# Layer-norm statistics of a gated cross-attention block: totals over partitions on TensorE, or on VectorE after copies by ScalarE

## The chip, the cores and the metric

The kernel runs on one core of a Trainium2 chip. A core has five engines that run side by side, each through its own instructions in order: TensorE for matrix products (PE in the profile; its weight loads are shown apart as PEld), VectorE (DVE), ScalarE (ACT), GpSimd (POOL) and SyncE (SP), which issues most DMAs. They wait for one another through semaphores. Working data lie in SBUF, products land in PSUM (eight banks); both have 128 partitions.

The metric is device time in microseconds (us): the median of three runs, and beside it one profiled execution from which all durations come.

## What is computed

`x` is 4 x 2048 tokens of 512 features, the context 4 x 77 rows of 384. Without the drawing of inputs and the splitting into 16 heads of 64 the reference is:

```python
def _layernorm(x, axis=-1, eps=1e-05):
    m = jnp.mean(x, axis=axis, keepdims=True)
    v = jnp.var(x, axis=axis, keepdims=True)
    return (x - m) / jnp.sqrt(v + eps)

# attention: softmax((x Wq)(ctx Wk)^T / 8) (ctx Wv) Wo + bo, softmax over the 77 context rows
x = x + jnp.tanh(g_xattn[0]) * _L0_xattn_ref(_layernorm(x, axis=-1), ctx_768, Wq, Wk, Wv, Wo, bo)
# FFN: one of eight matrices, picked by argmax(log_softmax(logits) + gumbel(u)): x W[idx] + b[idx]
x = x + jnp.tanh(g_ffn[0]) * _L0_ffn_ref(_layernorm(x, axis=-1), W, b, logits, u)
```

So every token is normalised twice: before the attention (here "x statistics") and before the FFN ("y statistics", of the attention's result).

## The kernel before, in words

**Weights are folded.** Wq and the keys are multiplied ahead into `m`, one matrix per batch row from the 512 features to 16 heads x 80 padded context rows; Wv and Wo into `vo`. Wq and W are centred, so the mean of a token need not be subtracted from it, and 1/std is applied after the product. What the norm has to deliver is therefore 1/std of each token: `rs`, and for the softmax `up` and `down`, 1/std times plus and minus 1/8.

**Groups.** The 8192 tokens go in 16 groups of 512. In the loop `for i in range(1, NGRP)` (from L802), step i computes the scores of group i, the attention of group j = i - 1 and the FFN of j, whose last product and row work fall into the next step, where that group is called f. Each of these is a Strassen-like product of seven block products instead of eight: class `Seven` (L458). `product(s)` puts block product s on PE, and `post(s)` moves a finished sum from PSUM. By `ORDER` (L460), products 0, 2, 4 and 6 add up in bank r = 0, products 1 and 5 in r = 1, product 3 in r = 2. Posts 0, 1, 2 and 6 are copies by ACT (`keep`, L485 or L489), posts 3, 4 and 5 additions by DVE into the copies in `snap` (L504). Since product 4 adds onto what is in bank 0, it can start only when post 2 has copied that bank; product 2 likewise waits for post 0, product 5 for post 1. The last group's attention and FFN use the order `BY_TOKENS`, where product 3 adds onto the bank that post 1 copies and product 4 onto that of post 2.

**Order.** The schedule is written by hand: each engine runs its instructions in the order in which the program lists them, so an instruction that waits holds all behind it on its engine.

**Layout and statistics.** A row tile holds 512 tokens: partition 32a + c holds feature piece a (128 of the 512 features) of tokens c, c + 32, and so on, 16 tokens along the free axis. `bn_stats` on DVE (L375) gives for each partition and token two triples (count, mean, 64 times the variance) of the even and the odd elements. Each token's eight means and eight variances thus lie on four partitions, 32 apart, and must be combined over them. The class `Norms` (L361) does it in four steps:

- `mean`: DVE adds the two means (L379), and PE multiplies with `jm` (L384), a constant of 0.125 wherever the partitions agree modulo 32. Each partition then has the token's mean, in the PSUM bank `stat`.
- `spread` and `var`: DVE subtracts it from the piece means, squares, adds the variances (L399 to L403) and adds pairs (L379); PE multiplies with `jm` again (L384).
- `rstd`: DVE adds eps (L412), POOL raises to the power -0.5 (L415 for x, L422 for y) and makes `down` and `up` (L418, L419).

`apart` separates DVE's additions from the product (`flush`), so that PE need not wait. There are 19 such objects: groups 0 and 1 before the loop (x only, n = 16 columns), groups 2 to 15 in the loop (y of group f and x of group i together, n = 32), and three at the end (the y of group 14, n = 16, and the two halves of group 15, `n1` and `n0`, n = 8).

**Where they stand.** For groups 0 and 1 the steps are in the loop over `s1` of group 0 (L710 to L733), which also centres and scales the FFN weights (`centre_wf`, `scale_wf`: L655 to L663). In the loop, `mean` comes after the seventh product of `s0` (L844) and the other steps at s = 1 to 3 of the scores `s1` and `s2` (L848). At the end they are in the last attention (L970 to L982, and L998 to L1000) and in the last FFN (L1026 to L1045). There the FFN rows are scaled by `rs` (L1018 on ACT, L1063 on DVE) and added to `y` (L1022, DVE), and the result is stored by halves.

Of the kernel before, what the change touches and what calls it, by code (L numbers as in the profile page):

```python
# [8 lines left out]
F32 = mybir.dt.float32  # L9
U32 = mybir.dt.uint32  # L10
AF = mybir.ActivationFunctionType
ALU = mybir.AluOpType
AX = mybir.AxisListType
# [6 lines left out]
def flamingo_block_kernel(  # L20
# [79 lines left out]
    tq = cp.tile([P, 4, NDC // 2, T2], F32, tag="tq")  # L100
    bo_c = cp.tile([P, NDC], F32, tag="bo_c")
    bf_r = cp.tile([P, P], F32, tag="bf_r")
    jm = cp.tile([P, NA, 32], F32, tag="jm")
    ones = cp.tile([P, P], F32, tag="ones")
    neghalf = cp.tile([P, NG], F32, tag="neghalf")
    snap = cp.tile([P, NCC * ID], F32, tag="snap")
# [79 lines left out]

    nc.gpsimd.memset(neghalf, -0.5)
    nc.gpsimd.memset(ones, 1.0 / D)
    nc.gpsimd.memset(jm, 0.0)
    for a in range(NA):  # L190

        for a2 in range(NA):
            nc.gpsimd.affine_select(
                out=jm[:, a, :], in_=jm[:, a, :], compare_op=ALU.not_equal, fill=0.125,
                base=-32 * a2, pattern=[[-1, 32]], channel_multiplier=1)

    def by_chunk(t):

# [162 lines left out]
    class Norms:  # L361


        apart, waiting = False, None

        def __init__(self, i, n=None):
            self.y = 2 <= i
            self.x = i < NGRP
# [5 lines left out]
            for g in range(g0, g0 + n):  # L374
                nc.vector.bn_stats(self.s6[:, at + g, :], t[:, g, :])  # L375

        def total(self, pairs, half):
            t = small.tile([P, self.n], F32, tag=f"tot{half}", name="tot")
            nc.vector.tensor_reduce(t, pairs, AX.X, ALU.add)  # L379
            self.waiting = half, t  # L380

        def flush(self):
            half, t = self.waiting
            nc.tensor.matmul(self.ps[:, half], jm.rearrange("p a c -> p (a c)"), t, start=True, stop=True)  # L384

        def mean(self):
            n = self.n
            self.ps = stat[:, : 2 * n].rearrange("p (h n) -> p h n", h=2)
            self.mm = self.s6.rearrange("p g (h s) -> p g h s", h=2)
            self.total(self.mm[:, :, :, 1], 0)  # L390
            if not self.apart:
                self.flush()

        def spread(self):
            n = self.n
            sq = stat[:, ds(4 * NG, 2 * n)].rearrange("p (n h) -> p n h", h=2)
            dv = small.tile([P, n, 2], F32, tag="dv", name="dv")
            for t in (dv, sq):
                nc.vector.tensor_tensor(t, self.mm[:, :, :, 1],  # L399
                                        self.ps[:, 0].unsqueeze(2).to_broadcast([P, n, 2]), ALU.subtract)  # L400
            nc.vector.tensor_tensor(sq, sq, dv, ALU.mult)
            self.q = small.tile([P, n, 2], F32, tag="q", name="q")
            nc.vector.scalar_tensor_tensor(self.q, self.mm[:, :, :, 2], 1.0 / 64, sq, ALU.mult, ALU.add)  # L403

        def var(self):
            self.total(self.q, 1)
            if not self.apart:
                self.flush()

        def rstd(self):  # L410
            self.rs = small.tile([P, self.n], F32, tag="rs", name="rs")
            nc.vector.tensor_scalar(self.rs, self.ps[:, 1], EPS, None, ALU.add)  # L412
            if self.x:
                r = self.rs[:, ds(self.x0, NG)]
                nc.gpsimd.tensor_tensor(r, r, neghalf, ALU.pow)  # L415
                self.up = small.tile([P, NG], F32, tag="up", name="up")
                self.down = small.tile([P, NG], F32, tag="down", name="down")
                nc.gpsimd.tensor_scalar(self.down, r, -SCALE, None, ALU.mult)  # L418
                nc.gpsimd.tensor_scalar(self.up, r, SCALE, None, ALU.mult)  # L419
            if self.y:  # L420
                r = self.rs[:, : min(self.n, NG)]
                nc.gpsimd.tensor_tensor(r, r, neghalf[:, : min(self.n, NG)], ALU.pow)  # L422

    def to_columns(dst, src, q):
        nc.vector.transpose(dst[:, q, :].rearrange("p (g c) -> p g c", c=32), src[:, :, ts(q, 32)])  # L425
# [112 lines left out]
    nmx = {}  # L538

    def head_max(i, h):  # L540
        mx = stat[:, ds((8 + h) * NG, NG)]
        nc.vector.tensor_reduce(mx, head(i, h), AX.X, ALU.max)  # L542
        nmx[h] = small.tile([P, NG], F32, tag=f"nmx{h}", name="nmx")
        nc.vector.tensor_tensor(nmx[h], mx, norms[i].down, ALU.mult)  # L544
# [127 lines left out]
        ff.post(6)  # L672

    def norm_step(n, s):
        if s < 4:
            (n.mean, n.spread, n.var, n.rstd)[s]()

    def early_step(n, s):

        if s == 0:  # L680
            n.apart = True
            n.mean()
        elif s == 1:
            n.flush()
            n.spread()
            n.var()
        elif s == 2:
            n.flush()
            n.rstd()


    n = norms[0]
# [17 lines left out]
    for s in range(7):  # L710
        s1.product(s)
        if s == 0:
            s1.post(0)
            s0.product(6)
            s0.post(6)
            early_step(n, 0)
            for k in range(2):
                s_rows(0, KH + k, s0.chunk(1, k))
            sum_wf(wfr)
        elif s < 3:  # L720
            early_step(n, s)
            n1.stats(xg[1], 0, 8 * (s - 1), 8)
        elif s < 6:
            early_step(n1, s - 3)
        if 0 < s:
            s1.post(s)
        if s == 4:
            centre_wf(wfr)
        if s == 5:
            scale_wf(wfr)  # L730
            for k in range(2):
                s_rows(0, 2 + k, s1.chunk(0, k))
# [69 lines left out]
    for i in range(1, NGRP):  # L802
# [4 lines left out]
        if 1 < i:  # L807

            s0 = scores0(i)
            for s in range(6):  # L810
                s0.product(s)
                if s == 0:
                    s0.post(0)
                    if 0 <= f:
                        end_of_ff(f)
                    p_columns(j, 6, 8)
                    xc[i].sum("T4")
                if s == 1:
                    p_columns(j, 8, 10)
                    if 0 <= f:  # L820
                        f_rows(f, ff, 1)
                if s == 2:
                    pT[j].sum("T1")
                    pT[j].sum("T3")
                if 0 < s:
                    s0.post(s)
                if 0 <= f and s in (2, 3):
                    n.stats(ys[f], 0, 8 * (s - 2), 8)
                if s == 3 and 0 <= f:
                    add_bias(f, nc.gpsimd)  # L830
            for k in range(2):
                s_rows(i, k, s0.chunk(0, k))

# [2 lines left out]
            for s in range(7):  # L836
                s1.product(s)
                s2.product(s)
                if s == 0:
                    s1.post(0)  # L840
                    s2.post(0)
                    s0.product(6)
                    s0.post(6)
                    n.mean()  # L844
                    for k in range(2):
                        s_rows(i, KH + k, s0.chunk(1, k))
                elif s < 4:
                    norm_step(n, s)  # L848
                if swap_vo and 3 <= s:
                    weight_sum(vo, s - 3, nc.vector if s < 5 else None)  # L850
                if 5 <= s and 0 <= f:
# [108 lines left out]
    for s in range(7):  # L960
# [7 lines left out]
            pT[j].sum("T3")  # L968
            n.stats(ys[f], 0, 0, NG)
        if s == 1:  # L970
            n.apart = True
            n.mean()
            add_bias(f, nc.vector)
        if s == 2:
            n.flush()
            n.spread()
            n.var()
            pT[j].sum("T4")
        if s == 3:
            n.flush()  # L980
            n.rstd()
            f_scale(f, n.rs, 0, 8)  # L982
        if s == 4:
            residual(j, at, "12")
# [9 lines left out]
        if s == 6:  # L994
            yc[j].sum("T3")
            residual(j, at, "11")
            y_rows(j, 2, 1)
            n1.stats(ys[j], -8, 8, 8)  # L998
            n1.apart = n0.apart = True
            n1.mean()  # L1000
            y_rows(j, 0, 0)
            residual_last(j, at)
    yc[j].sum("T1")
# [13 lines left out]
        for g in range(NG // 2):  # L1017
            nc.scalar.activation(d[:, g, :], d[:, g, :], AF.Copy, scale=rs[:, g : g + 1])  # L1018

    def added(h, v):  # L1020
        y = by_feature(ys[j], h, v)
        nc.vector.tensor_tensor(y, y, by_feature(ts_[j], h, v), ALU.add)  # L1022

    for s in range(6):
        ff.product(s)
        if s == 0:  # L1026
            n1.flush()
            n1.spread()
            n1.var()
            y_rows(j, 2, 0)  # L1030
            n0.stats(ys[j], 0, 0, 8)
        if s == 1:
            n1.flush()
            n1.rstd()
            yc[j].sum("T4")
            n0.mean()
            half_bias(1, nc.vector)
        if s == 2:
            n0.flush()
            half_bias(0, nc.gpsimd)  # L1040
            n0.spread()
            n0.var()
        if s == 3:
            n0.flush()
            n0.rstd()  # L1045
        ff.post(s)
        if s == 3:
            f_rows(j, ff, 0, 1)
            scaled(0, 1, n1.rs)
        if s == 4:  # L1050
            f_rows(j, ff, 1, 1)
            added(0, 1)
            scaled(1, 1, n1.rs)
        if s == 5:
            f_rows(j, ff, 0, 0)
            scaled(0, 0, n0.rs)
            added(1, 1)
            store(j, 8, 8, (nc.sync, nc.sync, nc.sync, nc.scalar))
    ff.product(6)
    for k in range(2):  # L1060
        to_rows(ts_[j], ff.ps[0][:, k, :], 2 + k, 0)
    d = by_feature(ts_[j], 1, 0)
    nc.vector.tensor_tensor(d, d, n0.rs.unsqueeze(2).to_broadcast(list(d.shape)), ALU.mult)  # L1063
    added(0, 0)
    added(1, 0)
    store(j, 0, 8, (nc.sync, nc.scalar))


# [39 lines left out]
```

## Time and profile before

| | |
|---|---|
| Three runs | 1263.02, 1263.13, 1263.99 us; median 1263.13 |
| The profiled execution | 1261.51 us; span from first to last instruction 1259.6 us; granted TensorE clock 0.998 |
| Statistics products on PE (L384) | 38 products, 76 records, 0.256 us median each |
| Powers on POOL | L415: 16 of 128x16, median 2.91 us, longest 4.09; L422: 15 of 128x16, 2.93; 2 of 128x8, 2.71 and 1.65 |
| Small operations of `spread` (128x64) on DVE | L399 0.20 and 0.23, L401 0.23, L403 0.24, L379 0.22 us |
| A small copy on ACT (L310, 128x80) | 0.23 us long, the next copy starts after 0.12 |
| DVE's addition of 128x512 (L1022), POOL's (L576) | 0.69 us, 1.27 us |
| One group of the loop, from product to same product | 72.97 us |

The page divides the span into 40 slices of 31.5 us and gives each engine's busy share in tenths; "PEclk" is the clock granted to TensorE, 9 meaning full speed. The chain of work that ended last is followed back from the last instruction, at each step to what released it. A row of a timeline gives start, duration, engine, line, operation, what is written and read, the shapes, how many like instructions are merged, and in brackets how long the engine was idle before and what ended that.

### The profile page before, as it was taken

Reading aid. Unit: us, or ns where it says so; the run is one execution under the profiler, and the core shown is the slowest. Engines: PE = TensorE matmul, PEld = TensorE weight load, DVE = VectorE, ACT = ScalarE, POOL = GpSimd, SP = SyncE. Lnnn points to the kernel's source line nnn. Section 1 sums busy time; section 2 is a strip of 40 time slices with the busy share of each in tenths; the row PEclk is TensorE's granted clock in tenths of the full one; section 3 lists DMA queues with packets and bytes.
Section 4 is the critical chain, followed back from the end, with each engine's and each line's share of the span. In section 5 each row is a group of like instructions: output and inputs, shape, how many; then the busy total and the mean of one; then the engine's idle time right before and its main releaser. Section 6 shows DMA issues by size and latency. Waiting matters only on the chain.

```text
span 1259.6 us, 16932 instructions
## 1 busy us (share of the span) xinstructions
PE 1246.9 (99%) x5780; PEld 1067.7 (85%) x5780; DVE 886.2 (70%) x1858; ACT 639.1 (51%) x1748; POOL 879.0 (70%) x483
## 2 busy tenths in 40 slices
PE   9999999999999999999999999999999999999996
PEld 6575888888888888888888888888888888888885
DVE  5789876667777676777766767766766787666566
ACT  3539453719265372926446292744628273563813
POOL 5352895866957786676968687675976697575764
PEclk9999999999999999999999999999999999999999
DMA  9766400314014030303106030212304120010102
GB/s 271 291 199 214 114 1 1 68 42 109 1 28 124 1 67 1 68 22 98 32 1 151 1 68 1 46 22 84 67 1 110 42 56 11 2 34 1 34 1 67
DMA packets 95221, 80.28 MB, mean 64 GB/s; under 512 B 3856, under 2 KB 83088, under 8 KB 95136
## 3 DMA queue, kind: packets, MB, share of 16 engines
q1 hardware_dynamic: 92768, 76.74, 24.0%
q10 hardware_dynamic: 1760, 1.34, 0.3%
q8 instruction: 46, 0.75, 0.3%
q0 software_dynamic: 608, 1.13, 0.2%
q14 instruction: 39, 0.32, 0.1%
HBM read 44.07 MB, written 35.13 MB: 63 GB/s over the span
## 4 chain that ended last, share of the span: by engine, by line
PE 96%; DVE 2%; ACT 1%; issue 0%; POOL 0%; DVEq 0%; ACTq 0%
PE ps_s L479 38%; PE ps_a L479 37%; PE ps_f L479 15%; PE ps_kv L274 2%; PE ps_vo L339 2%; PE ps_m L304 2%; PE ps_st L384 0%; ACT t L604 0%; PE ps_w L168 0%; ACT t L1018 0%; DVE s L375 0%; DVE snap L504 0%; POOL rs L422 0%; DVE vo L342 0%; DVE y L430 0%
## 5 line engine op out<-in xcount | busy, mean ns | idle before, releaser
L479 PE MATMUL ps_a<-pT,vo 128*128 128x256 f32 x2240 | 486.7, 379 | 0.0
L479 PEld LDWEIGHTS ps_a<-pT,vo 128*128 128x128 f32 x2240 | 425.5, 190 | 57.8
L550 ACT ACTIVATE s<-s,nmx,up 128x77 f32<-128x77 f32 x1024 | 355.6, 446 | 0.4 <-DVE nmx L544 0.3
L479 PE MATMUL ps_s<-tq,m 128*128 128x256 f32 x1280 | 294.2, 381 | 0.2 <-ACT snap L485 0.2
L450 POOL TENSOR_TENSOR pT<-pT 128x1280 f32<-128x1280 f32 x64 | 185.8, 2904 | 125.3 <-PE ps_a L479 111.7
L479 PEld LDWEIGHTS ps_s<-tq,m 128*128 128x128 f32 x1280 | 241.3, 190 | 35.8 <-issue 3.2
L485 ACT COPY snap<-ps_s 128x512 f32<-128x512 f32 (+1 forms) x188 | 93.8, 511 | 306.8 <-DVE t L430 131.4
L479 PE MATMUL ps_s<-xc,m 128*128 128x256 f32 x960 | 222.7, 381 | 0.0
L479 PEld LDWEIGHTS ps_s<-xc,m 128*128 128x128 f32 x960 | 180.8, 190 | 28.2 <-DVE vo L342 2.4
L561 POOL TENSOR_TENSOR s<-s,sm 128x1232 f32<-128x1232 f32 x64 | 145.1, 2268 | 65.9 <-DVE sm L558 46.1
L504 DVE TENSOR_TENSOR snap<-snap,ps_s 128x512 f32<-128x512 f32 (+1 forms) x141 | 83.5, 593 | 82.0 <-PE ps_s L479 82.0
L533 DVE STREAM_TRANSPOSE s<-snap 128x512 f32<-128x512 f32 x156 | 99.9, 685 | 46.8 <-ACT snap L485 44.8
L604 ACT ACTIVATE t<-t,rs 128x128 f32<-128x128 f32 x240 | 73.3, 389 | 100.7 <-POOL rs L422 100.7
L479 PE MATMUL ps_f<-tq,wf 128*128 128x256 f32 x512 | 118.7, 379 | 0.0
L570 DVE STREAM_TRANSPOSE pT<-s 128x512 f32<-128x512 f32 x160 | 101.0, 677 | 17.1 <-POOL s L561 17.1
L415 POOL TENSOR_TENSOR rs<-rs,neghalf 128x16 f32<-128x16 f32 x16 | 50.2, 3135 | 87.9 <-DVE rs L412 87.9
L450 POOL TENSOR_TENSOR tq<-xc,tq 128x512 f32<-128x512 f32 x64 | 85.2, 1332 | 34.9 <-PE ps_f L479 32.4
L479 PEld LDWEIGHTS ps_f<-tq,wf 128*128 128x128 f32 x512 | 97.0, 190 | 13.1
L557 DVE TENSOR_REDUCE sm<-s 128x16 f32<-128x1232 f32 x64 | 91.4, 1429 | 20.5 <-ACT s L550 20.5
L542 DVE TENSOR_REDUCE ps_st<-s 128x16 f32<-128x1232 f32 x64 | 92.4, 1444 | 2.1
L479 PE MATMUL ps_f<-xc,wf 128*128 128x256 f32 x384 | 90.8, 379 | 0.0
L450 POOL TENSOR_TENSOR tq<-xc 128x512 f32<-128x512 f32 x64 | 81.4, 1271 | 10.7 <-DVE xc L425 9.4
(126 smaller groups left out, 1137.7 us busy)
## 6 DMA issues: line engine op xcount, KB each, us to landing
xg<-in_x_dram SPq DMA_DIRECT2D x64, 256.0 KB, 5.8
out_dram<-y SPq DMA_DIRECT2D x60, 256.0 KB, 4.3
vo<-vo_d SPq DMA_DIRECT2D x16, 640.0 KB, 6.5
vo_d<-vo SPq DMA_DIRECT2D x16, 512.0 KB, 4.3
m<-m_d SPq DMA_DIRECT2D x12, 640.0 KB, 4.2
m_d<-vo SPq DMA_DIRECT2D x4, 960.0 KB, 7.9
wq<-in_WqT_dram SPq DMA_DIRECT2D x8, 256.0 KB, 6.5
wq<-in_Wo_dram SPq DMA_DIRECT2D x1, 2048.0 KB, 13.8
```

Source lines behind the costliest of these rows:

```text
L415: nc.gpsimd.tensor_tensor(r, r, neghalf, ALU.pow)
L450: (engine or nc.gpsimd).tensor_tensor(self.at[name], self.at[a], self.at[b_], op)
L479: nc.tensor.matmul(self.ps[r][:, n, :], self.w(blk, c, pair), self.cols(cname, c), start=(first and n == 0 and c == 0), stop=(c == h - 1), ...
L485: nc.scalar.copy(dst, self.ps[r])
L504: nc.vector.tensor_tensor(c, c, self.ps[r], ALU.add)
L533: nc.vector.transpose(key_chunk(sc[i], k), cols.rearrange("p (g h r) -> p g h r", h=HA, r=R))
L542: nc.vector.tensor_reduce(mx, head(i, h), AX.X, ALU.max)
L550: nc.scalar.activation(head(i, h)[:, g, :], head(i, h)[:, g, :], AF.Exp, scale=norms[i].up[:, g : g + 1], bias=nmx[h][:, g : g + 1])
L557: nc.vector.tensor_reduce(sm, head(i, h), AX.X, ALU.add)
L561: nc.gpsimd.tensor_tensor(head(i, h), head(i, h), sums[h].unsqueeze(2).to_broadcast([P, NG, J]), ALU.mult)
L570: nc.vector.transpose(pT[i].all[:, k, :].rearrange("p (g h r) -> p g h r", h=HA, r=R), key_chunk(sc[i], k))
L604: nc.scalar.activation(ts_[f][:, g, :], ts_[f][:, g, :], AF.Copy, scale=rs[:, g : g + 1])
```

## The change

It takes the products with `jm` out of `Norms`, and `jm` itself. In their place are three steps:

- `gather`: eight copies by ACT (two for each of the four feature pieces) bring all piece means and variances of a token side by side onto partitions 0 to 31, the means into the PSUM bank `stat`, the variances into `m2` in SBUF.
- `calc` and `power`: DVE adds and squares there, on 32 partitions, with eight values a token along the free axis; POOL raises to -0.5, 16 columns at a time.
- `back`: four ACT copies bring 1/std to the four groups of partitions; POOL then makes `down` and `up`.

The steps' places change: in the loop `gather` comes ahead of the transposes of the first scores, `calc` and `power` where `mean` was, `back` at s = 3. Before the loop they take the first, second and third place of the old steps. In the last FFN the ACT scalings of one quarter become one DVE product, and two of the four additions to `y` go from DVE to POOL. The scratch of `head_max` moves within `stat`.

```diff
-        def total(self, pairs, half):
...
-        def flush(self):
-            half, t = self.waiting
-            nc.tensor.matmul(self.ps[:, half], jm.rearrange("p a c -> p (a c)"), t, start=True, stop=True)
...
+        def gather(self):
+
+            self.mean = stat[:32, : 8 * self.n].rearrange("p (n e) -> p n e", e=2 * NA)
+            self.m2 = small.tile([32, self.n, 2 * NA], F32, tag="m2", name="m2")
+            parts = self.s6.rearrange("p g (h s) -> p g h s", h=2)
+            for a in range(NA):
+                for to, k in ((self.mean, 1), (self.m2, 2)):
+                    nc.scalar.copy(to[:, :, ts(a, 2)], parts[ts(a, 32), :, :, k])
+
+        def calc(self):
+            def tile_of(shape, name):
+                return small.tile([32, self.n] + shape, F32, tag=name, name=name)
+
+            tot, dv, self.r = tile_of([], "tot"), tile_of([2 * NA], "dv"), tile_of([], "r32")
+            nc.vector.tensor_reduce(tot, self.mean, AX.X, ALU.add)
+            wide = tot.unsqueeze(2).to_broadcast([32, self.n, 2 * NA])
+            for to in (dv, self.mean):
+                nc.vector.scalar_tensor_tensor(to, wide, -0.125, self.mean, ALU.mult, ALU.add)
+            nc.vector.tensor_tensor(self.mean, self.mean, dv, ALU.mult)
+            nc.vector.scalar_tensor_tensor(dv, self.m2, 1.0 / 64, self.mean, ALU.mult, ALU.add)
+            nc.vector.tensor_reduce(tot, dv, AX.X, ALU.add)
+            nc.vector.tensor_scalar(self.r, tot, 0.125, EPS, ALU.mult, ALU.add)
+
+        def power(self):
+            for at in range(0, self.n, NG):
+                r = self.r[:, at : min(at + NG, self.n)]
+                nc.gpsimd.tensor_tensor(r, r, neghalf[:32, : r.shape[1]], ALU.pow)
+
+        def back(self):
             self.rs = small.tile([P, self.n], F32, tag="rs", name="rs")
-            nc.vector.tensor_scalar(self.rs, self.ps[:, 1], EPS, None, ALU.add)
+            for a in range(NA):
+                nc.scalar.copy(self.rs[ts(a, 32)], self.r)
...
     def norm_step(n, s):
-        if s < 4:
-            (n.mean, n.spread, n.var, n.rstd)[s]()
...
         if s == 0:
-            n.apart = True
-            n.mean()
+            n.gather()
         elif s == 1:
-            n.flush()
-            n.spread()
-            n.var()
+            n.calc()
+            n.power()
         elif s == 2:
-            n.flush()
-            n.rstd()
+            n.back()
...
+            n.gather()
             for k in range(2):
                 s_rows(i, k, s0.chunk(0, k))
...
-                    n.mean()
+                    n.calc()
+                    n.power()
                     for k in range(2):
                         s_rows(i, KH + k, s0.chunk(1, k))
-                elif s < 4:
-                    norm_step(n, s)
+                elif s == 3:
+                    n.back()
...
+    def scaled_at_once(h, v, rs):
+        d = by_feature(ts_[j], h, v)
+        nc.vector.tensor_tensor(d, d, rs.unsqueeze(2).to_broadcast(list(d.shape)), ALU.mult)
+
+    def added(h, v, engine):
...
         if s == 0:
-            n1.flush()
-            n1.spread()
-            n1.var()
+            n1.calc()
+            n1.power()
             y_rows(j, 2, 0)
             n0.stats(ys[j], 0, 0, 8)
+        ff.post(s)
+        if s == 0:
+            n0.gather()
         if s == 1:
-            n1.flush()
-            n1.rstd()
             yc[j].sum("T4")
-            n0.mean()
+            n0.calc()
             half_bias(1, nc.vector)
+            n1.back()
         if s == 2:
-            n0.flush()
             half_bias(0, nc.gpsimd)
-            n0.spread()
-            n0.var()
+            n0.power()
         if s == 3:
-            n0.flush()
-            n0.rstd()
-        ff.post(s)
+            n0.back()
```

The last lines of that function then read:

```diff
         if s == 4:
             f_rows(j, ff, 1, 1)
-            added(0, 1)
-            scaled(1, 1, n1.rs)
+            added(0, 1, nc.gpsimd)
         if s == 5:
             f_rows(j, ff, 0, 0)
             scaled(0, 0, n0.rs)
-            added(1, 1)
+            scaled_at_once(1, 1, n1.rs)
+            added(1, 1, nc.vector)
...
-    added(0, 0)
-    added(1, 0)
+    scaled_at_once(1, 0, n0.rs)
+    added(0, 0, nc.gpsimd)
+    added(1, 0, nc.vector)
```

## The prediction

> **What bounds the kernel now.** I read the page first: engine shares, the granted clock by slice, the chain that ended last.
>
> ```profile
> PE 1246.9 (99%) x5780; PEld 1067.7 (85%) x5780; DVE 886.2 (70%) x1858; ACT 639.1 (51%) x1748; POOL 879.0 (70%) x483
> ...
> PEclk9999999999999999999999999999999999999999
> ...
> PE 96%; DVE 2%; ACT 1%; issue 0%; POOL 0%; DVEq 0%; ACTq 0%
> ```
>
> PE is busy throughout at full clock and is 96% of the chain. So an edit pays by the PE time it removes, and costs when it makes PE wait. DVE, ACT and POOL have 30 to 50% free, so their work matters only where PE stands behind it. Next, PE's timeline around the statistics' products of one group.
>
> ```profile
> 196.81 1.89 PE L479 MATMUL ps_s<-tq,m 128*128 128x256 f32 x8
> 198.54 0.30 PE L384 MATMUL ps_st<-tot,jm 128*128 128x32 f32 x2
> 198.68 5.43 PE L479 MATMUL ps_s<-tq,m 128*128 128x256 f32 x24
> 203.94 0.30 PE L384 MATMUL ps_st<-tot,jm 128*128 128x32 f32 x2
> 204.08 2.84 PE L479 MATMUL ps_s<-xc,m 128*128 128x256 f32 x12
> ```
>
> Eight ordinary records take 198.54 - 196.81 = 1.73 us, 0.216 each. A statistics product (two records) takes 198.68 - 198.54 = 0.14, and the 24 records behind it take 5.26 where 24 x 0.216 = 5.18: 0.08 more. Each product costs PE 0.22 us, not the 0.30 of its row.
>
> **The loop: -6.2 us.** Groups 2 to 15 have two products each: 28 x 0.22 = 6.2. The question is whether the new work holds PE there; I follow group 2. *Gather* (eight ACT copies): stats end at 193.2, ACT is idle from 189.8 to 196.54. A small ACT copy is not in the trace at 32 partitions; nearest is L310 (128x80, 0.23 long, the next copy starts 0.12 after it), furthest L550's pointer form (0.45). I take 0.12: done by 194.3. *Calc* takes the place of L379 at 196.37, where DVE then waits until 199.41 for ACT's copy of the seventh product. It is seven operations of 32 x 8 = 256 elements a partition: rows are 0.24 (128x64, L403) and 0.42 (128x256, L504), so at most about 2.8 us for seven, against 3.0 free. The old five small operations behind it (1.1 us) vanish. *Power*: two POOL operations of 128x16, 2.93 each now; POOL works on add_bias until 197.82, so they run 199.2 to 205.1. *Back* (four ACT copies) stands ahead of the posts at s = 3, which are DVE's, and ACT has nothing else before the last posts at 213.91: about 8 us of cover. If the cover were gone, those posts would hold the attention products' banks. `down` and `up` come at about 206 (207.57 now), the scaling of the FFN rows earlier by 5 us; neither is waited for by PE. So the loop keeps its 6.2.
>
> **Removing jm: 0.** Its sixteen selects end at 5.3 us; POOL then waits for DVE until 10.62 anyway.
>
> **The opening: +5.1 us.** Here `back` stands ahead of a post that PE needs. From the timeline between 74 and 91 us:
>
> ```profile
> 77.25 1.31 DVE L533 STREAM_TRANSPOSE s<-snap 128x512 f32<-128x512 f32 x2 [1.12 <-ACT snap L485]
> ...
> 78.64 1.07 ACT L485 COPY snap<-ps_s 128x512 f32<-128x512 f32 x2 [1.43 <-DVE s L533]
> ...
> 81.13 2.94 POOL L415 TENSOR_TENSOR rs<-rs,neghalf 128x16 f32<-128x16 f32 x1 [1.34 <-DVE rs L412]
> ...
> 81.54 1.89 PE L479 MATMUL ps_s<-tq,m 128*128 128x256 f32 x8
> ...
> 85.81 3.31 ACT L662 ACTIVATE wf<-wfr,tg 128x256 f32<-128x256 f32 x8 [6.10 <-DVE wfr L657]
> ...
> 89.03 1.30 ACT L485 COPY snap<-ps_s 128x512 f32<-128x512 f32 x3
> 89.91 0.73 PEld L479 LDWEIGHTS ps_s<-tq,m 128*128 128x128 f32 x4 [0.40 <-ACT snap L485]
> ```
>
> The row at 78.64 is posts 1 and 2 of `s1`. Product 4 (81.54) adds onto the bank that post 2 copies, so it can't start before post 2 ends. Now post 2 queues on ACT behind `back`, which waits for POOL's power, which waits for calc. Calc can start when DVE is done with the transposes, 78.55: seven operations of 128 elements, from L403's 0.24 (64) and L504's 0.42 (256) about 0.3 each with 0.035 between dependent ones, two of them overlapped: 2.05 -> 80.6. Power 2.94 -> 83.55. Back 0.5 -> 84.05. Post 2 0.55 -> 84.6. Product 4 starts at 84.6 instead of 81.54, and PE stands from about 80.2. The wait goes on: ACT gathers group 1's pieces only now, 0.95 -> 85.45 (the stats are done at about 83.8); calc 2.05 -> 87.5; power 2.95 -> 90.5; back 0.5 -> 91.0. Behind `back` on ACT stand the eight scalings L662 (85.81 to 89.03: 3.22) -> 94.2, then post 6 of `s1` (0.46) and post 0 of `s2` (0.37) -> 95.05. `s2`'s third product waits for that post already now (the last line, 89.91): it moves by 95.05 - 89.91 = 5.1 us. From there to 118 us PE has no gap in which to make it up. The removed products are inside these absolute times.
>
> Bounds: power on 32 partitions between 1.65 (128x8, L422) and 4.09 (the longest 128x16); I take 2.94, since elements a partition are those of that row. Calc between 1.4 (the old operations' 0.2 each) and 2.9 (seven of 0.42). Copies 0.12 to 0.23 (one after the other). Power and calc count twice, copies 16 times: the opening costs 1.2 to 8.9, mostly 3 to 7.
>
> The page "TensorE: Matmul & The Clock Gate" (Part 1) says that an idle window of about 3.4 us lets the array's clock fall to half until PE has been busy as long. Before shows no such pause: its longest gap after the start is 0.87 us, its clock 0.998. Its first six records (L168) took 4.12 us from 1.45 to 5.57 where twelve of 0.216 are 2.6: a cold start of 1.5 us. By the rule the 4.4 us pause may bring that again, and the sum would be about 0 instead of -1.4.
>
> **The end: -0.3 us.** From the last 50 us:
>
> ```profile
> 1242.42 2.71 POOL L422 TENSOR_TENSOR rs<-rs,neghalf 128x8 f32<-128x8 f32 x1 [3.91 <-DVE rs L412]
> ...
> 1242.78 1.97 PE L479 MATMUL ps_f<-xc,wf 128*128 128x256 f32 x8
> ...
> 1248.65 1.65 POOL L422 TENSOR_TENSOR rs<-rs,neghalf 128x8 f32<-128x8 f32 x1
> ...
> 1252.95 1.29 DVE L1022 TENSOR_TENSOR y<-y,t 128x512 f32<-128x512 f32 x2
> 1254.28 0.89 ACTq L612 DMA_DIRECT2D out_dram<-y  x2
> ```
>
> Times here are counted from the start of the last attention. Its two products go (-0.45), the sixth's post comes 1.5 earlier as the row scaling is done sooner, so stats of the first half end at 1236.0 (1237.5 now), and PE starts the last FFN at 1235.9. Calc of n1 1237.5 to 1239.1, y_rows and stats of n0 to 1241.5. ACT, after post 0, stands for these stats, gathers (0.95), gives n1 back (0.5) and only then does post 1, until 1243.4. Product 3 adds onto post 1's bank: 1243.4 instead of 1242.78, and PE ends 0.25 later than now. But DVE's tail is shorter: eight ACT scalings (2.0) become one DVE product (0.69) and two of the four additions go to POOL. DVE: post 5 at 1248.8 (0.68), transposes 0.77, scale 0.69, add 0.65, transposes 0.77, scale 0.69, add 0.65: 1253.7, against 1254.24. POOL's last addition (1.27, L576) follows ACT's eight scalings (1250.2 to 1252.2): 1253.5 undisturbed. The output DMAs stay as they are. -0.55 if POOL is undisturbed, up to +0.5 if not; I take -0.3.
>
> That not comes from the rows: of POOL's powers, 2.71 ran beside DVE's bias addition, 1.65 beside a shorter addition. "GPSIMD Engine Reference" (Specifications) says POOL's SBUF interface is shared with VectorE and suffers from DVE instructions with two SBUF inputs, which both of DVE's last two are; the rows agree once and disagree once. By the rule the end is +0.5 and the sum -0.6.
>
> **Sum.** -6.2 + 5.1 - 0.3 = -1.4 us on the profiled execution's own 1261.51 (span 1259.6 and 1.9 around it): 1260.1. The three runs' median is 1.6 above that execution, so 1263.13 - 1.4 = 1261.7. About 0.2% (2.5 us) is what a measurement of this kernel can tell from no change; -1.4 is inside.
>
> **Rivals.**
> 1. *The opening's wait is shorter.* Power at 1.65 and calc at 1.4 take 2 x 1.3 + 2 x 0.65 = 3.9 off: 1257.8. For it: a quarter of the partitions. Against: times here follow elements a partition (IOTA 32x4 0.13, 128x8 0.14).
> 2. *No wait in the opening at all*, only products removed: -6.2 - 2.2 (four products and waits of 0.87 and 0.4) - 0.3 = -8.7: 1254.4. It needs post 2 or product 4 not to be in the order that I read; against it, ACT's rows follow the program's order.
> 3. *Slower: ACT's small copies cost more than their spacing.* Sixteen stand in the opening's chain, twelve ahead of the end's post 1. At c us each the sum is -1.4 + 28 x (c - 0.12): zero at 0.17, 0.2% slower from 0.26, +7.8 at L550's 0.45 (1270.9); with 0.27, 1265.9. For it: reads of a strided 24-byte record across partitions, which no row shows. Against: L310's row. A cold clock would add 1.5 to any of these.
>
> **Chances.** Forecast (change between -2.5 and +2.5) 0.45; rival 1 0.24; rival 2 0.11; rival 3 or a longer wait of another kind 0.20. Faster 0.35, same 0.45, slower 0.20. The forecast's own range is 1260.6 to 1265.6; the range to hold 8 in 10 takes in rival 1 and the start of 3: 1256.7 to 1265.9.
>
> **What would show it.** No L384 row, and 72.5 us from group to group (72.97 now): loop right. A PE pause of about 4 us at 80 behind ACT's post, a second near 92.5: opening right; no pause: rival 2. Gather's copies 0.12 apart, power 2.9: prices right. A granted clock under 9 in the third slice: the cold start. A pause of 2 us ahead of product 3 in the last FFN, and POOL or DVE ending the last addition before 1254: end right. New gaps of PE in every group would make the prediction wrong, 14 times over.

## The result: 1.75 us slower, and the profile after

The changed kernel takes 1265.03 us (median of 20 runs, 1264.13 to 1266.91), the kernel before 1263.28 (20 runs, 1261.47 to 1264.01). The ratio is 1.0016, 95% interval 1.0010 to 1.0022: +1.75 us, where -1.4 was forecast. The profiled execution of the changed kernel took 1265.61 us, with a span of 1263.8.

From its page, the rows that stood at the head of the prediction:

```profile
PE 1244.6 (98%) x5704; PEld 1064.5 (84%) x5704; DVE 914.7 (72%) x1857; ACT 686.3 (54%) x1968; POOL 874.6 (69%) x468
...
PEclk9989999999999999999999999999999999999998
...
PE 94%; DVE 3%; ACT 1%; POOL 1%; issue 0%; DVEq 0%; ACTq 0%
```

The 76 records are gone (5780 to 5704), and PE is busy 2.3 us less, but it is 94% of the chain instead of 96, and in the third and the last slice its clock was not full. A table of stretches, from the starts of the records on PE in each trace, shows where the time went (the stretch ahead of the first scores is left out: it took 54.4 to 56.9 us in the profiles of this study, with the same instructions on PE):

| us | before | changed |
|---|---|---|
| first scores of group 0 to the `vo` products behind its last scores (the opening) | 40.06 | 46.43 |
| from there to the first attention | 47.14 | 47.14 |
| first attention to that of group 14 (14 groups) | 1021.88 | 1015.63 |
| to the start of the last FFN | 72.97 | 72.52 |
| last FFN, to the end of PE | 13.76 | 16.83 |
| end of PE to end of span | 9.39 | 9.54 |

The loop gave -6.25, group 14's statistics -0.45; the opening took back 6.37 and the end 3.22. The sum, +2.9, is that of two single executions; the medians differ by 1.75.

The granted clock, given with each execution as a mean, also differs among the 20 of the changed kernel: 0.993 to 0.995 in 16 of them, with a median time of 1265.34 us, and 0.997 in four, with 1264.26 (0.998 in the profile before). So the low clock that is described next goes with about 1.1 us; without most of it the change still costs about 1 us.

The opening, in picked rows of the changed kernel's timeline (L374 is `gather`, L398 is `back`, L393 the power, L467 a post's copy, L644 the scaling of the FFN weights):

```profile
80.04 0.58 ACT L467 COPY snap<-ps_s 128x512 f32<-128x512 f32 x1
81.98 2.94 POOL L393 TENSOR_TENSOR r<-r,neghalf 32x16 f32<-32x16 f32 x1 [0.86 <-DVE r L388]
84.95 0.84 ACT L398 COPY rs<-r 32x16 f32<-32x16 f32 x4 [4.33 <-POOL r L393]
85.81 0.58 ACT L467 COPY snap<-ps_s 128x512 f32<-128x512 f32 x1
86.45 3.78 PE L461 MATMUL ps_s<-tq,m 128*128 128x256 f32 x8 [4.55 <-ACT snap L467]
89.77 2.91 POOL L393 TENSOR_TENSOR r<-r,neghalf 32x16 f32<-32x16 f32 x1 [3.42 <-DVE r L388]
92.71 0.84 ACT L398 COPY rs<-r 32x16 f32<-32x16 f32 x4 [4.89 <-POOL r L393]
93.58 3.30 ACT L644 ACTIVATE wf<-wfr,tg 128x256 f32<-128x256 f32 x8
96.79 1.09 ACT L467 COPY snap<-ps_s 128x512 f32<-128x512 f32 x3
97.67 1.13 PE L461 MATMUL ps_s<-tq,m 128*128 128x256 f32 x4 [0.20 <-ACT snap L467]
```

This reads from top to bottom as the chain that the prediction worked out: post 1, power, ACT standing 4.33 us for it, `back`, post 2, and PE's product 4 after a pause of 4.55 us; then the same again for group 1, and the last scores' third product behind ACT's scalings. The eight records of product 4 took 3.78 us instead of 1.89. The same execution by stretches gives the granted clock (a row gives the stretch and its length, then the busy time of PE, PEld, DVE, ACT and POOL with the number of instructions, and last the clock, the DMA share and GB/s):

```profile
80.00:86.40 6.40, 1.90 (x9) 1.33 (x7) 5.33 (x24) 2.01 (x8) 4.53 (x4) 0.95 0.89 165
86.40:90.00 3.60, 3.55 (x8) 2.86 (x9) 1.76 (x7) 1.35 (x8) 0.23 (x1) 0.50 0.00 0
90.00:94.00 4.00, 4.00 (x12) 2.63 (x11) 2.71 (x5) 1.23 (x6) 3.04 (x3) 0.68 0.00 0
```

After the pause PE ran at half clock for some 6 us: 3.6 us at 0.50, and a mean of 0.68 over the next 4 us is half clock for 2.6 of them. The prediction named this fall (the Trainium skill, "TensorE: Matmul & The Clock Gate", Part 1: an idle window of about 3.4 us) and left it out of the sum. The trace agrees for this pause of 4.55 us; the end, below, shows that one of 2.63 us can be enough. The second pause that was forecast, near 92.5, is only 0.20 us here (before 97.67), because PE worked through its products at half clock.

The end, from the same timeline (L998 is an addition to `y`):

```profile
1243.55 0.17 ACT L374 COPY ps_st<-s 32x16 f32<-32x16 f32 x1 [3.49 <-DVE s L365]
...
1244.82 0.57 ACT L467 COPY snap<-ps_f 128x512 f32<-128x512 f32 x1
...
1245.41 0.82 ACT L398 COPY rs<-r 32x8 f32<-32x8 f32 x4
...
1245.44 3.05 PE L461 MATMUL ps_f<-xc,wf 128*128 128x256 f32 x8 [2.63 <-ACT snap L467]
...
1248.29 2.56 PE L461 MATMUL ps_f<-tq,wf 128*128 128x256 f32 x8
...
1256.35 1.66 POOL L998 TENSOR_TENSOR y<-y,t 128x512 f32<-128x512 f32 x1 [2.80 <-ACT t L990]
1256.99 1.56 DVE L998 TENSOR_TENSOR y<-y,t 128x512 f32<-128x512 f32 x1
```

ACT waits for the stats, gathers until 1244.8, only then does post 1, and product 3 stands 2.63 us; `back` (1245.41) comes behind that post. Products 3 and 4 then last 2.85 and 2.40 us from start to start instead of 1.73: the granted clock is 0.50 here from 1246.23 to 1249.65. And the last two additions, now one each on POOL and DVE, lengthen each other: 1.56 on DVE, where one alone takes 0.69.

### The profile page after: what moved, and what is told of

Same layout as the page of the kernel before. It is cut to its first block, busy times and chain, and to the rows that moved or that the text cites. A ratio compares the mean times of both kernels' runs of the same rounds, so it can differ in the third digit from the quotient of the medians.

```text
span 1263.8 us, 16986 instructions
## 1 busy us (share of the span) xinstructions
PE 1244.6 (98%) x5704; PEld 1064.5 (84%) x5704; DVE 914.7 (72%) x1857; ACT 686.3 (54%) x1968; POOL 874.6 (69%) x468
## 4 chain that ended last, share of the span: by engine, by line
PE 94%; DVE 3%; ACT 1%; POOL 1%; issue 0%; DVEq 0%; ACTq 0%
PE ps_s L461 37%; PE ps_a L461 36%; PE ps_f L461 15%; PE ps_kv L266 2%; PE ps_vo L331 2%; PE ps_m L296 2%; POOL r L393 1%; DVE s L365 1%; PE ps_w L167 0%; ACT t L586 0%; ACT snap L467 0%; ACT wf L644 0%; DVE r L388 0%; DVE vo L334 0%; DVE t L412 0%
## 5 line engine op out<-in xcount | busy, mean ns | idle before, releaser
L461 PEld LDWEIGHTS ps_s<-tq,m 128*128 128x128 f32 x1280 | 243.9, 191 | 42.1 <-ACT snap L467 6.3
L467 ACT COPY snap<-ps_s 128x512 f32<-128x512 f32 (+1 forms) x188 | 93.5, 514 | 287.5 <-DVE t L412 131.1
L393 POOL TENSOR_TENSOR r<-r,neghalf 32x16 f32<-32x16 f32 (+1 forms) x33 | 94.0, 2857 | 22.2 <-DVE r L388 21.8
L461 PEld LDWEIGHTS ps_f<-xc,wf 128*128 128x128 f32 x384 | 73.6, 192 | 13.0 <-ACT snap L467 3.0
```

What stands on the lines that cost most here:

```text
L393: nc.gpsimd.tensor_tensor(r, r, neghalf[:32, : r.shape[1]], ALU.pow)
L461: nc.tensor.matmul(self.ps[r][:, n, :], self.w(blk, c, pair), self.cols(cname, c), start=(first and n == 0 and c == 0), stop=(c == h - 1), ...
L467: nc.scalar.copy(dst, self.ps[r])
```

## The experiments

The theory to be tested: the loop gains its full 6.2 us; ACT's order (a copy that waits, ahead of a post that PE needs) loses it in the opening and at the end. The rivals: the new work itself is what costs (copies, 32-partition operations, POOL); the low clock is what costs. "Before" was run beside each; ratios are to it.

**1. The loop alone.** Opening and end get back the old class and its order (called `OldNorms`), word for word as in the kernel before.

```diff
-    norms[0] = Norms(0)
+    norms[0] = OldNorms(0)
...
-    n = norms[NGRP] = Norms(NGRP)
-    n1, n0 = Norms(NGRP + 1, NG // 2), Norms(NGRP + 2, NG // 2)
+    n = norms[NGRP] = OldNorms(NGRP)
+    n1, n0 = OldNorms(NGRP + 1, NG // 2), OldNorms(NGRP + 2, NG // 2)
```

> The new statistics in the loop alone; opening and end as before (products with jm, old last additions). Theory (PE time saved in the loop, lost again by ACT's order in the opening and at the end): 14 groups x 0.45 us, so 6.2 us under before, 1257.0, and 72.52 us from group to group. Rival (the copies and the 32-partition work slow something everywhere): less than half of that, 1260 or more.

Measured 1256.96 us (1255.99 to 1258.18), ratio 0.9951 (0.9937 to 0.9964). The stretch of 14 groups took 1015.64 us, 72.52 from group to group but for the exchanges of weights (72.64). The loop's gain is the whole of PE's removed time; nothing in it waits for the new work.

**2. and 3. Opening or end as before, the rest changed.** The same edit in one place only.

> Opening as before, loop and end new. Theory: the opening's stall goes (6.4 us longer in the changed kernel's trace than in the one before, start of the clock left out), so about 1259: the end alone is lost, some 2 us. Rival that the end is where all of it is lost: 1264 or more.

> Opening and loop new, end as before. Theory: -6.2 from the loop, +6.4 from the opening: 1263.4. If opening and end do not add up (a stall in one hides in the other): under 1261 or over 1265.

With the old opening: 1258.16 us (1256.79 to 1258.53), ratio 0.9956 (0.9943 to 0.9970); the opening took 40.06 us, as before. With the old end: 1262.62 us (1261.54 to 1264.66), ratio 0.9996 (0.9987 to 1.0005); the opening took 46.45. Against the loop alone the new opening thus costs 5.7 us and the new end 1.2. Together they would make 1263.8; the changed kernel took 1265.03, so about 1.2 us of it does not come out of this sum of medians.

**4. The same work in the opening, behind the posts.**

```diff
         elif s < 3:
-            norm_step(n, s)
+            if s == 1:
+                norm_step(n, 1)
             n1.stats(xg[1], 0, 8 * (s - 1), 8)
-        elif s < 6:
-            norm_step(n1, s - 3)
         if 0 < s:
             s1.post(s)
+        if s == 2:
+            norm_step(n, 2)
+        if s == 3:
+            norm_step(n1, 0)
...
             for k in range(2):
                 s_rows(0, 2 + k, s1.chunk(0, k))
+            norm_step(n1, 1)
...
     s_rows(0, KH + 4, s2.chunk(1, 0))
+    norm_step(n1, 2)
```

> The changed kernel with one thing moved: in the opening, the copies back to 128 partitions of group 0 stand behind post 2 instead of ahead of it, group 1's gather behind post 3, its calc behind the FFN weights' work, its copies back behind the last scores. No work is left out. Theory (the order on ACT, not the copies): product 4 does not wait, no pause of PE of 4 us near 80 us, clock at full speed in that slice; 5.5 to 6.5 us under the changed kernel, about 1259. Rival (the copies' own time or POOL's power): within 1 us of the changed kernel, 1264 to 1266.

Measured 1258.33 us (1257.40 to 1258.52), ratio 0.9959 (0.9945 to 0.9972): 6.7 us under the changed kernel with the same instructions. The opening took 40.20 us instead of 46.43, which is 6.2 of them. From PE's timeline of this kernel, the opening (first two rows) and the last FFN (last two):

```profile
82.07 1.89 PE L461 MATMUL ps_s<-tq,m 128*128 128x256 f32 x8
...
91.78 1.13 PE L461 MATMUL ps_s<-tq,m 128*128 128x256 f32 x4 [1.49 <-ACT snap L467]
...
1239.54 1.99 PE L461 MATMUL ps_f<-xc,wf 128*128 128x256 f32 x8 [2.63 <-ACT snap L467]
1241.37 1.89 PE L461 MATMUL ps_f<-tq,wf 128*128 128x256 f32 x8
```

Product 4 (82.07) has no wait and full speed: the cause of its pause is the order on ACT, for copies, calc and power are all still there. A remainder of 1.49 us stands ahead of the third product of the last scores, since ACT's gather for group 1 and the scalings still precede its post. The end is the changed kernel's, with its pause of 2.63 us, and in this profile the clock did not fall: the products took 1.83 and 1.72.

**5. PE kept busy in the opening's pause.** The products added compute nothing that is used.

```diff
+    def keep_busy(n):
+        ps = bank("ps_w")
+        for _ in range(n):
+            nc.tensor.matmul(ps[:, :T2], m[:, 0, 0, 0, :], xc[0]("B11", 0), start=True, stop=True)
...
     for s in range(7):
+        if s == 4:
+            keep_busy(10)
         s1.product(s)
```

> The changed kernel with ten more products (128x256, into a PSUM bank that nobody reads) on PE ahead of product 4 in the opening, where PE now stands 4.5 us and then ran eight records in 3.57 instead of 1.73 us. No output changes. Theory (the opening's length is ACT's chain: back, gather, calc, power, back, scalings, posts; PE has 2 us to spare in it): granted clock 1.0 there, but the third product of the last scores starts as late as now, time within 0.7 us of the changed kernel, 1264.3 to 1265.7. Rival (the low clock itself costs the opening some 3 us): 1262.5 or less.

Measured 1267.80 us (1266.21 to 1268.13), ratio 1.0034 (1.0022 to 1.0046): 2.8 us over the changed kernel, outside both expectations. PE's timeline of it:

```profile
87.04 1.99 PE L461 MATMUL ps_s<-tq,m 128*128 128x256 f32 x8 [0.24 <-ACT snap L467]
...
94.05 1.03 PE L461 MATMUL ps_s<-tq,m 128*128 128x256 f32 x4
98.27 1.93 PE L461 MATMUL ps_s<-tq,m 128*128 128x256 f32 x4 [3.20 <-ACT snap L467]
99.99 1.91 PE L461 MATMUL ps_s<-xc,m 128*128 128x256 f32 x4
```

Product 4 now runs at full speed, and PE simply comes to the next wait for ACT earlier and stands 3.20 us there. The opening is ACT's chain, as expected: the third product of the last scores starts 41.93 us after the first scores here and 41.91 in the changed kernel, so there the half clock was hidden in it. What I had not expected is that the clock then falls behind the second pause, where nothing hides it: four records take 1.72 us from start to start instead of 0.86, twice. That is the opening's 48.13 us against 46.43, 1.7 of the 2.8; the rest stays open.

**6. PE kept busy in the end's pause.** Six such products on FFN data ahead of product 3.

```diff
     for s in range(6):
+        if s == 3:
+            keep_busy(6)
         ff.product(s)
```

> The changed kernel with six such products ahead of product 3 of the last FFN, where PE now stands 2.6 us. No output changes. Theory: the wait for ACT's post 1 stays (PE resumes at the same time), but the two products behind it run at full speed, 1.72 each instead of 2.85 and 2.40, and from there PE sets the end: 1.0 to 1.8 us under the changed kernel where its clock fell, so median 1263.3 to 1264.2. Rival (the end is set by ACT, DVE and POOL, not PE): within 0.5 of 1265.

Measured 1264.53 us (1263.07 to 1265.47), ratio 1.0009 (1.0000 to 1.0018): 0.5 under the changed kernel, less than expected, and on the edge of the rival. In its profile product 3 starts as late as ever, but products 3 and 4 take 1.83 and 1.73 us, and the last FFN's PE time is 15.15 us instead of 16.83. The end of the kernel gained 1.3 of these 1.7. The clock's price at the end is thus up to 1.3 us in an execution in which it falls, and it does not fall in every one (run 4).

**7. The end's order altered: gather and copies back behind post 2.**

```diff
-        ff.post(s)
-        if s == 0:
-            n0.gather()
         if s == 1:
             yc[j].sum("T4")
-            n0.calc()
             half_bias(1, nc.vector)
+        ff.post(s)
+        if s == 2:
+            n0.gather()
             n1.back()
-        if s == 2:
             half_bias(0, nc.gpsimd)
-            n0.power()
-        if s == 3:
-            n0.back()
         if s == 3:
             f_rows(j, ff, 0, 1)
             scaled(0, 1, n1.rs)
+            n0.calc()
+            n0.power()
         if s == 4:
             f_rows(j, ff, 1, 1)
             added(0, 1, nc.gpsimd)
+            n0.back()
```

> The changed kernel with the end's order alone altered: n0's gather and n1's copies back behind post 2 of the last FFN, n0's calc and power behind the first transposes, n0's copies back at s = 4. No work is left out. Theory: product 3 does not wait, the clock stays up: 2.3 to 2.9 us under the changed kernel, 1262.1 to 1262.7. Rival (the dearer scaling chain of n0 takes the place of the wait): 1264 or more.

Measured 1265.53 us (1263.99 to 1266.15), ratio 1.0018 (1.0009 to 1.0027): a miss. The wait was moved, not removed. From its timeline:

```profile
1243.12 1.89 PE L461 MATMUL ps_f<-xc,wf 128*128 128x256 f32 x8
...
1243.29 1.26 POOL L432 TENSOR_TENSOR tq<-xc,tq 128x512 f32<-128x512 f32 x1
...
1243.85 4.09 DVE L985 TENSOR_TENSOR y<-y,bf_r 128x1024 f32<-128x1024 f32 x1
...
1244.52 2.34 POOL L985 TENSOR_TENSOR y<-y,bf_r 128x1024 f32<-128x1024 f32 x1
...
1251.56 3.65 PE L461 MATMUL ps_f<-tq,wf 128*128 128x256 f32 x8 [3.10 <-DVE snap L486]
```

Product 3 starts at 1243.12 without a wait. But DVE's bias addition, 1.21 us in both kernels, took 4.09: it ended 1.08 us after POOL's second addition (1244.52 + 2.34 = 1246.86). Post 3 stood behind it, and so on to product 6, which waited 3.10 us for DVE and ran at low clock.

**8. The same, both bias additions on DVE.**

```diff
-            half_bias(0, nc.gpsimd)
+            half_bias(0, nc.vector)
```

> The kernel with the end's order altered (1265.5), and the second bias addition of 128x1024 on DVE instead of POOL. Theory (there, DVE's bias addition took 4.09 instead of 1.21 us because POOL's ran at the same time, and held post 3 behind it): 1.2 us each, product 6 waits 1 us at most instead of 3.1, last FFN 1.5 to 3 us shorter, median 1262.5 to 1264. Rival (DVE is simply over-full there): 4 us of DVE lateness again, 1265 or more.

Measured 1264.13 us (1263.09 to 1265.90), ratio 1.0010 (1.0001 to 1.0019): 1.4 under the last, at the upper edge of what was expected. The two additions on DVE:

```profile
1243.32 2.92 DVE L985 TENSOR_TENSOR y<-y,bf_r 128x1024 f32<-128x1024 f32 x2
...
1249.86 2.77 PE L461 MATMUL ps_f<-tq,wf 128*128 128x256 f32 x8 [1.92 <-DVE snap L486]
```

Both together took 2.92 us where one took 4.09 beside POOL's, so POOL held DVE up. But product 6 still waits 1.92 us for DVE (1 at most was expected), which has both additions, calc and posts to do: the rival, an over-full DVE, holds in part.

**9. The order of the last additions alone**, on the kernel of run 1.

```diff
-            added(0, 1)
-            scaled(1, 1, n1.rs)
+            added(0, 1, nc.gpsimd)
...
-            added(1, 1)
+            scaled_at_once(1, 1, n1.rs)
+            added(1, 1, nc.vector)
...
-    added(0, 0)
-    added(1, 0)
+    added(0, 0, nc.gpsimd)
+    added(1, 0, nc.vector)
```

> The kernel with the new statistics in the loop alone (1257.0), and of the change's end only the last scalings and additions: one quarter's scalings by one DVE product, two additions on POOL. Theory (the last additions on DVE and POOL run side by side and hold each other up: in the changed kernel's trace 1.56 on DVE and 1.66 on POOL, where 0.69 and 1.27 are the rows alone): no gain, PE's end to the kernel's end 9.4 to 9.6 us as in both kernels, time 1256.5 to 1257.5. Rival (the new order pays and only the waits ahead of it cost): 0.6 us or more under, 1256.4 or less.

Measured 1257.34 us (1256.81 to 1257.78), ratio 0.9952 (0.9939 to 0.9966); the loop alone took 1256.96. No gain. In the profile the time from PE's end to the kernel's is 10.17 us, 0.74 more than the 9.43 of run 1 (9.4 to 9.6 was expected). Its last microseconds (L1088 is an addition, L1129 the last scaling):

```profile
1245.26 1.40 POOL L1088 TENSOR_TENSOR y<-y,t 128x512 f32<-128x512 f32 x1
...
1245.57 1.64 DVE L1088 TENSOR_TENSOR y<-y,t 128x512 f32<-128x512 f32 x1
...
1247.47 1.26 POOL L1088 TENSOR_TENSOR y<-y,t 128x512 f32<-128x512 f32 x1 [0.81 <-POOL y L1088]
1248.00 1.28 DVE L1129 TENSOR_TENSOR t<-t,rs 128x512 f32<-128x512 f32 x1
```

Each time DVE's operation (0.65 to 0.69 alone) ends about 0.55 us after POOL's, which is hardly lengthened (1.40 and 1.26): by these times DVE does its work when POOL is done.

**10. and 11. Better versions.** Run 10 has the end of run 7, and in the opening group 1's statistics are moved further, behind the last scores and into the next stage:

```diff
         s2.post(s)
+        if s == 2:
+            norm_step(n1, 0)
...
         exps(0, e[s], e[s + 1])
+        if s == 1:
+            norm_step(n1, 1)
+        if s == 4:
+            norm_step(n1, 2)
```

> As end_behind, and in the opening group 0's copies back behind post 2, group 1's gather behind post 2 of the last scores, its calc, power and copies back in the next stage. No work is left out. Theory: the loop's 6.2 stay, the opening gains the removed products and their waits, 1.5 to 2, the end 0 to 0.7: 1254.5 to 1256, under every kernel so far. If group 1's late statistics hold the next stage (head maxima of group 1 need them only 40 us on): 1257 or more.

Measured 1259.56 us (1258.19 to 1260.72), ratio 0.9973 (0.9962 to 0.9983): 3.6 us over the range that was expected. The opening took 39.66 us, but the stage behind it 48.32 instead of 47.14: there the `vo` products that start at 109.81 take 4.21 us to the next product, behind a wait for DVE, where they take 3.02 in run 4. In the 12 us around them DVE is busy for 11.74 us and ACT for all 12. The end is that of run 7.

Run 11 has run 4's opening, with the weights' scaling moved, group 14's statistics new, and group 15's halves and additions as before:

```diff
         if s == 5:
-            scale_wf(wfr)
...
         s2.post(s)
+        if s == 2:
+            scale_wf(wfr)
```

> A version from what the runs showed: new statistics in the loop, in the opening and for group 14's y; in the opening nothing of them ahead of a post that PE waits for, and the eight scalings of the FFN weights behind post 2 of the last scores; group 15's two halves and the last additions as before (products with jm). No work is left out. Expected: opening 1.5 to 2.7 us shorter than before, loop -6.2, group 14 -0.45, end as before: 1253.8 to 1255.2. If the opening gains nothing: 1256.5.

Measured 1255.53 us (1255.01 to 1256.40), ratio 0.9939 (0.9926 to 0.9953), the fastest of the study, 0.3 us over the range that was expected. The last FFN took 13.39 + 9.42 us and the 14 groups 1015.63. The opening gained 0.5 (39.59), not 1.5 to 2.7:

```profile
89.24 1.89 PE L533 MATMUL ps_s<-tq,m 128*128 128x256 f32 x8
...
94.60 1.13 PE L533 MATMUL ps_s<-tq,m 128*128 128x256 f32 x4 [0.88 <-DVE snap L558]
```

The third product of the last scores (in the row at 89.24) no longer waits for ACT, but the seventh waits 0.88 us for DVE, behind calc: again a wait that took another's place.

## Why the prediction was wrong, step by step

**What bounds the kernel, and the loop: right.** -6.2 forecast, -6.25 measured; all covers that were named held, 72.52 from group to group against 72.5 forecast.

**The opening: mechanism right, a term mis-sized.** +5.1 forecast, +6.37 measured. Pause, place and order were as worked out (4.4 us forecast, 4.55 seen), power 2.94 and 2.91 as assumed, calc 2.1. The step that failed is "I take 0.12" for a small ACT copy. The rows of `gather`:

```profile
78.50 0.20 ACT L374 COPY ps_st<-s 32x32 f32<-32x32 f32 x1
78.63 0.23 ACT L374 COPY m<-s 32x32 f32<-32x32 f32 x1
78.89 0.19 ACT L374 COPY ps_st<-s 32x32 f32<-32x32 f32 x1
```

After the copy into PSUM the next starts 0.13 us later, after the copy into SBUF 0.26: 0.39 a pair. This first `gather` does not hold up the chain, since DVE is at its transposes until 79.94 anyway, but group 1's does: it starts at 86.30, and calc behind it at 87.68, 1.38 us where 0.95 was forecast. `back` took 0.84 instead of 0.5, twice. Together 0.43 + 0.34 + 0.34 = 1.1 us of the 1.27 that were missed; the rest lies in smaller pieces. That the clock would fall was weighed at 1.5 us; it fell, and cost nothing there, because ACT's chain set the opening (run 5).

Three slips in the working change little: 84.6 + 0.95 is 85.55 and not 85.45; with all three terms at their dearest the opening would cost 10.9 us and not 8.9; and the longest pause of PE in the rows of before, its start left out, is 0.71 us (ahead of 79.48) and not 0.87.

**The end: wrong.** Forecast -0.3 with group 14's -0.45 in it; measured +2.77 in the profiled execution (-0.45 + 3.07 + 0.15). Three steps failed. First, PE's end was put 0.75 us later from the start of the last FFN; without a fall of the clock it is 1.39 (15.15 in runs 4 and 6 against 13.76). Product 3 starts 7.97 us after the FFN's start, 7.5 were forecast: the second half's statistics end at 5.99 instead of 5.6, `gather` starts 0.09 after them and takes 1.27 instead of 0.95 up to post 1, and that post 0.62 instead of 0.45 up to the product. Against this, the prediction misread the order: it put `back` of n1 (0.5 us) ahead of post 1, and in the kernel it stands behind it. Second, the clock: it was weighed for the pause of 4.4 us in the opening alone. The shorter one, 2.63, lowers it too, in some executions, and there PE sets the end: 1.68 us of PE time. Third, "two of the four additions go to POOL" was to shorten the tail by 0.8 us; it was the step that the rule on the shared interface spoke against (the Trainium skill, "GPSIMD Engine Reference", Specifications), and "the rows agree once and disagree once" let me take nearly the undisturbed value. Run 9 shows a loss of 0.74 instead.

**The sum.** With a fall of the clock at the end the terms give -6.25 + 6.37 + 2.77 = +2.9, without it -6.25 + 6.37 - 0.45 + 1.39 + 0.55 = +1.6 (0.55: end of PE to end of span 9.94 in run 4 against 9.39). The executions at a clock of 0.993 to 0.995 are 2.1 us over the median before, those at 0.997 1.0 us: the step between them is there, but both sums come out some 0.7 us too high, and that stays open.

**The chances.** 0.45 was on a change within 0.2%, which it is, but its sign is the other one: the loop came out as worked out, and opening and end were both put too low. The third rival, that ACT's copies cost more than their spacing, is part of what happened: at 0.20 a copy its formula gives +0.8.

## What to carry to other kernels

Work taken off the bounding engine pays in full only where the work put in its place stands behind nothing that this engine waits for: in a hand-written order, look at what queues behind each new waiting instruction, and place it behind the copies that free the banks. A regular loop with slack took the change without loss, while opening and end, where each post is just in time, gave all of it back; it was best to change the loop and keep the old way in the last group. An operation moved from DVE to POOL to halve a tail gained nothing here, since the two then ran at the same time on SBUF data (run 9).

## What the runs showed of the hardware

- DVE operations with two SBUF inputs waited for a POOL addition under way, rather than share with it: 4.09 us instead of 1.21 beside two POOL additions, 1.64 and 1.28 instead of 0.65 to 0.69 beside one, ending 0.55 to 1.1 us after POOL's end each time. A DVE addition with one input in PSUM kept its 0.69 beside one (the changed kernel at 1252.61), and one with two SBUF inputs that started together with a POOL power took 0.75 (before at 1248.65).
- The same pause of PE of 2.63 us was followed by low clock in the profiles of the changed kernel and of run 2, and by full clock in run 4's. The traces show why. In all 13 profiles, read in stretches of 0.1 us, the granted clock is 0.50 or 1.00 and changes only at times that lie whole multiples of 3.41 us apart (in the changed kernel at 85.70, 92.53, 1246.23 and 1249.65). Behind the first 20 us it fell after every such interval in which PE stood for 2.17 us or more, and after none with 1.67 or less; in between, 1.92 brought it down and 1.97 and 1.98 did not. A pause that is divided by one of these times does less: run 10's of 3.10 us (1.53 and 1.56) and run 4's (1.10 and 1.53) left the clock up, while run 8's of 1.92, inside one interval, did not.
- A PE pause that is filled to keep the clock up can make a kernel slower: the clock fell at the next pause, where it counted (run 5: an opening of 48.13 us instead of 46.43).
- Eight small ACT copies of 32 partitions take 1.54 us, 0.39 a pair, although each is no longer than the 0.23 of a copy of 128x80, which let the next start after 0.12.
